# Layernorms computed beside attention: statistics, scalings and turns gathered at query tiles 1 to 5 of two heads each, and x of the second batch loaded in four groups

## The chip, the cores and the metric

The kernel runs on one core of one Trainium2 chip. The metric is the device time of one execution in microseconds (us), the median over several runs. A smaller time is better.

## What is computed

One transformer block in float32 with adaptive layernorms, on x of 2 batches x 1024 rows x 256 columns. Six vectors per batch (a shift, a scale and a gate for each of the two halves) come from a small product with the conditioning vector.

```
h = layernorm(x) * (1 + ca) + sa
x = x + ga * attention(h)        # 16 heads of 128, rotary q and k, causal softmax, output product with Wo
h = layernorm(x) * (1 + cb) + sb
x = x + gb * ffn(h)              # 256 -> 704 (silu gate * up) -> 256, weights int32 minus 128, scaled
```

There are four layernorms in all: first ("a") and second ("b") of each batch. Layernorm a of batch 0 stands ahead of everything, b of batch 1 behind everything. The two in the middle, a of batch 1 and b of batch 0, are computed while the attention of other heads runs. These two are what the change is about.

## The kernel before, in words

**Units.** The attention runs in 32 units, one for each head of each batch (`units`, line 592): units 0 to 15 are the heads of batch 0, units 16 to 31 those of batch 1. The loop over units (line 695) holds a loop over the eight query tiles i of 128 rows (line 701). The order of the instructions on every engine is the order in which this code issues them; nothing is reordered behind it (`manual_schedule`, line 646).

**One query tile i of a unit.** TensorE first multiplies an attention output of an earlier head with Wo (`project_out`, L509), and VectorE adds the result into x (L512); there is a single PSUM buffer for this product, so the next one has to wait until VectorE has taken it. Then come the scores of the tile against keys 0 to i (`score`, L422). VectorE adds the mask and takes the row maximum (L425), ScalarE takes the exponential (`expo`, L442). VectorE then turns the probabilities of the tile before, i - 1, in blocks of 32 x 32 (`turned`, L456); those of a unit's tile 7 are turned at tile 0 of the next unit. At tiles 1, 3, 4 and 6 TensorE also projects a half of q or k of the next unit (`project_qk`, L379). ScalarE turns half of it round (L391), GpSimd multiplies and adds (L392, L398), VectorE adds the bias and multiplies by the cosine (L395, `release`).

**The turned probabilities travel.** Blocks of 32 x 32 are turned on VectorE; the exchange between partition groups is done by 16 DMAs for each half of the query tiles, issued from SP (L468). They start when tile 3 or tile 7 is turned. The value products (`values`, L483) of the second half of a unit begin at tile 5 of the next unit, right after that tile's scores, and those of the first half at tile 7 of its own unit.

**What runs beside it.** At the end of each tile the loop calls `extras(n, i)` (line 595), with n the unit. It issues weight folding on GpSimd, loads and scalings of the feed-forward weights, and the middle layernorms. The table `((14, 1, "a"), (30, 0, "b"))` (line 619) says that the first one is due in unit m = 14 and the second in unit m = 30. A layernorm of eight row tiles takes these steps:

- `ln_stats` (L185, L186): mean and variance of a tile, VectorE
- `ln_sqrt` (L190): one square root for all tiles, ScalarE; it needs another activation table than the exponential, so a table load stands ahead of it and ahead of the next exponential
- `ln_scale` (L198, L201): reciprocal, then subtraction and multiplication, VectorE
- `ln_move` (L228): a 32 x 32 turn, VectorE
- `ln_send` (L237): eight DMAs from SP at a time, 16 in all; `ln_shift` (L240): shift and scale, GpSimd

Before the change the statistics of the eight tiles are taken in unit m - 4 (10 and 26), one at each query tile 0 to 7. The square root comes at query tile 1 of unit m - 3 (11 and 27). A scaling is issued at each of tiles 2 to 7 of that unit and 0 and 1 of unit m - 2 (12 and 28); each turn comes one query tile after its scaling. The x of batch 1 is loaded by ScalarE's DMA queue, in two groups of four single tiles, at tile 7 of units 4 and 8 (`load_x`, L64).

Of the kernel before, what the change touches and what calls it, by code (L numbers as in the profile page):

```python
# [21 lines left out]
NT = S // P  # L22
# [15 lines left out]
def adaln_block(ctx: ExitStack, tc: tile.TileContext, a, cos_d, sin_d, out):  # L38
    nc = tc.nc
# [23 lines left out]
    def load_x(b, t, n, eng):  # L63
        eng.dma_start(x[b][:, t : t + n, :], x_d[b, :, t : t + n, :])  # L64
# [47 lines left out]
    def modulation(which, pool, tag):  # L112

        pm = pool.tile([P, 512], F32, tag=tag, name=f"pm{which}")
        for n in range(2):
            for f in range(KC):
                at = (n * KC + f) * B
                for k in range(KC):
                    nc.tensor.matmul(
                        pm[:, at : at + B],  # L120
                        wmod[:, which // 2, k, n * D + f * P : n * D + (f + 1) * P],
                        sc[:, :, k],
                        start=(k == 0),
                        stop=(k == KC - 1),
                    )
                if not which:
                    warm_up(1)
        pms[which] = pm
# [3 lines left out]
    def shift_scale(which):  # L132
        pm = pms[which]
        for n in range(2):
            nc.vector.tensor_scalar(
                modT[:, which + n].rearrange("p f b -> p (f b)"),
                pm[:, n * KC * B : (n + 1) * KC * B],
                float(n),
                None,
                ALU.add,  # L140
            )
# [36 lines left out]
    def ln_stats(b, name, t):  # L178
        if t == 0:
            stats[b, name] = (  # L180
                small.tile([P, NT, 2], F32, tag="mv", name=f"mv_{name}{b}", bufs=2),
                small.tile([P, NT], F32, tag="rstd", name=f"rstd_{name}{b}", bufs=2),
            )
        st = small.tile([P, 6], F32, tag="st", name=f"st_{name}{b}_{t}")
        nc.vector.bn_stats(st, x[b][:, t, :])  # L185
        nc.vector.bn_aggr(stats[b, name][0][:, t, :], st)  # L186

    def ln_sqrt(b, name, t0, t1):
        mv, rstd = stats[b, name]
        nc.scalar.activation(rstd[:, t0:t1], mv[:, t0:t1, 1], AF.Sqrt, bias=eps_t)  # L190
# [3 lines left out]
    def ln_scale(b, name, blk, part=range(4)):  # L194
        mv, rstd = stats[b, name]
        part = [4 * blk + j for j in part]
        some = slice(part[0], part[-1] + 1)
        nc.vector.reciprocal(rstd[:, some], rstd[:, some])  # L198
        for t in part:
            xn = xnp.tile([P, D], F32, tag="xn", name=f"xn_{name}{b}_{t}")  # L200
            nc.vector.tensor_scalar(  # L201
                xn, x[b][:, t, :], mv[:, t, 0:1], rstd[:, t : t + 1], ALU.subtract, ALU.mult
            )
            xns[b, name, t] = xn
# [16 lines left out]
    def ln_move(b, name, t):  # L221

        if t == 0:
            moved[b, name] = [
                fpool.tile([P, 4, NB, KC, 4, 32], F32, tag="f", name=f"xt{n}_{name}{b}") for n in range(2)
            ]

        nc.vector.transpose(  # L228
            moved[b, name][0][:, :, t // 4, :, t % 4, :].rearrange("p c f q -> p f c q"),
            xns[b, name, t].rearrange("p (f c a) -> p f c a", c=4, a=32),  # L230
        )

    def ln_send(b, name, cs):
        src, dst = moved[b, name]
        for c in cs:
            for r in range(4):
                nc.sync.dma_start(dst[ts(c, 32), r], src[ts(r, 32), c])  # L237

    def ln_shift(b, name, blk, which, dest, f):
        nc.gpsimd.tensor_scalar(  # L240
            dest[:, f, :].rearrange("p (j r q) -> p r j q", j=4, q=32),
            moved[b, name][1][:, :, blk, f],
            modT[:, which + 1, f, b : b + 1],
            modT[:, which, f, b : b + 1],
            ALU.mult,
            ALU.add,
        )
# [10 lines left out]
    def ffn_scale_load():  # L258
        t = fpool.tile([P, 2 * HID], F32, tag="f", name="s_bc")
        nc.scalar.dma_start(t, a["scales"][:, : 2 * HID].to_broadcast([P, 2 * HID]))  # L260
        sbc.update(gate=t[:, :FULL], up=t[:, FULL : 2 * FULL], last=t[:, 2 * FULL :])

    def ffn_weight_load(n):
        if n == "gate":
            t = fpool.tile([P, KC * 2 * HID], I32, tag="f", name="raw")
            at = 0
            for m, w in (("gate", FULL), ("up", FULL), ("last", P)):
                raws[m] = t[:, at : at + KC * w].rearrange("p (k h) -> p k h", k=KC)
                at += KC * w
        nc.scalar.dma_start(raws[n], a[f"wq_{n}"])  # L270

    def ffn_weight_scale(n, k):
        nc.vector.scalar_tensor_tensor(
            wT[n][:, k, :], raws[n][:, k, :], -ZERO_POINT, sbc[n], ALU.add, ALU.mult
        )

    def ffn_down_load():
        raws["down"] = fpool.tile([P, NF, D], I32, tag="f", name="raw_down")
        nc.scalar.dma_start(raws["down"], a["wq_down"])
        sbc["down"] = xnp.tile([P, D], F32, tag="xn", name="s_down")  # L280
        nc.scalar.dma_start(sbc["down"], a["scales"][:, 2 * HID :].to_broadcast([P, D]))

    def ffn_down_scale(b, c):

        if c == 0:
            sd = sbc["down", b] = xnp.tile([P, D], F32, tag="xn", name=f"sd{b}")
            nc.vector.tensor_tensor(sd, sbc["down"], gate["b", b], ALU.mult)
        nc.vector.scalar_tensor_tensor(
            wdT[b][:, c : c + 2, :],
            raws["down"][:, c : c + 2, :],  # L290
            -ZERO_POINT,
            sbc["down", b].unsqueeze(1).to_broadcast([P, 2, D]),
            ALU.add,
            ALU.mult,
        )
# [27 lines left out]
    def fold_out(b, g):  # L323
        t = weights[b, g]["o"]
        if b == 0:

            for h in range(HG):
                c = R_BV + g * HG + h
                bw = small.tile([P, D], F32, tag="bw", name=f"bw_{g}{h}", bufs=2)
                nc.gpsimd.tensor_scalar(bw, t[:, h, :], cols[:, c : c + 1], None, ALU.mult)  # L330
                nc.gpsimd.tensor_tensor(bvacc, bvacc, bw, ALU.add)

        for h in range(HG):
            nc.gpsimd.tensor_tensor(t[:, h, :], t[:, h, :], gate["a", b], ALU.mult)
# [260 lines left out]
    def extras(n, i):  # L595

        if i == (2 if n else 7) and units[n][2] == 0:
            fold_out(*units[n][:2])
        if n == 0 and i == 6:
            modulation(2, ps_a, "a")  # L600
            shift_scale(2)

        if n == 2 and i == 7:
            ffn_scale_load()
        for m, name in ((3, "gate"), (5, "up"), (6, "last")):
            if n == m and i == 7:
                ffn_weight_load(name)
            if n == m + 1 and i in (2, 5):
                ffn_weight_scale(name, i // 4)
        if n in (4, 8) and i == 7:  # L610
            for t in range(4):
                load_x(1, n - 4 + t, 1, nc.scalar)
        if n == 7 and i == 7:
            ffn_down_load()
        if n in (8, 9) and i in (1, 3, 5):
            ffn_down_scale(n - 8, i - 1)


        for m, b, name in ((14, 1, "a"), (30, 0, "b")):
            if n == m - 4:  # L620
                ln_stats(b, name, i)
            if n == m - 3 and i == 1:
                ln_sqrt(b, name, 0, NT)
            t = 8 * (n - m + 3) + i - 2
            if 1 <= t <= NT:
                ln_move(b, name, t - 1)
            if 0 <= t < NT:
                ln_scale(b, name, t // 4, (t % 4,))
            if n in (m - 2, m - 1) and i == 6:
                ln_send(b, name, ((0, 1), (2, 3))[n - m + 2])  # L630
            if n == m and i in (4, 5, 7):
                blk = i // 6
                if i != 5:
                    dest = (new_hT if b else new_h2)(b, blk)
                else:
                    dest = (hT if b else h2s)[b, blk]
                for f in {4: (0,), 5: (1,), 7: (0, 1)}[i]:
                    ln_shift(b, name, blk, 0 if b else 2, dest, f)
        if n == 14 and i == 5:
            bias_row()  # L640
        if n == 15:
            add_bias(0, i)
        if n == 20:
            add_bias(1, i)

    with tc.manual_schedule():
# [48 lines left out]
        for n, u in enumerate(units):  # L695
            b, g, h = u
# [142 lines left out]
```

## Time and profile before

| what | value |
|---|---|
| median of 3 runs | 1085.96 us (1085.74 to 1087.61) |
| the profiled execution's own time | 1085.72 us |
| its span, first to last instruction | 1083.9 us |
| granted TensorE clock | 1.000 |
| busy: TensorE, VectorE, ScalarE, GpSimd | 99%, 60%, 47%, 37% |
| start of unit 0's and of unit 31's scores | 24.2 us, 931.1 us |

In the profile PE is TensorE's matmuls, PEld its weight loads, DVE VectorE, ACT ScalarE, POOL GpSimd, SP the engine that only issues DMAs; L422 is line 422 of the kernel. The unit starts are the first score matmul of a unit: the score group has 768 records, 24 in each unit, in order of time. Offsets "after the unit's start" below count from there.

### The profile page before, as it was taken

The numbers are of one execution on the slowest core, as the hardware profiler recorded it, in microseconds if no ns is written. First come the engines' busy times: TensorE is split into PE (matmuls) and PEld (weight loads), VectorE is DVE, ScalarE is ACT, GpSimd is POOL, SyncE is SP. The second block draws the span as 40 slices with busy tenths as digits, with TensorE's granted clock in tenths as the row PEclk, the third lists the DMA queues.
The fourth block names the chain that finished last, engine by engine and source line by source line (L and its number), as shares of the span: only waits on it lengthen the run. The fifth ranks groups of instructions, "written<-read, shape, count | busy, mean of one in ns | idle before, by whom it ended". The sixth has DMA issues, their size and how long they took to land.

```text
span 1083.9 us, 12352 instructions
## 1 busy us (share of the span) xinstructions
PE 1072.0 (99%) x3524; PEld 638.7 (59%) x3524; DVE 655.5 (60%) x1422; ACT 507.6 (47%) x956; POOL 397.2 (37%) x364
## 2 busy tenths in 40 slices
PE   8999999999999999999999999999999999999998
PEld 5556555566666556556566666665655566555656
DVE  5566566767677856556656665666677766454321
ACT  4645445455445444445455444454445445652110
POOL 4635353535343343664343433333333334100000
PEclk9999999999999999999999999999999999999999
DMA  6355656657564556555564645454556556422001
GB/s 211 81 140 132 159 141 137 168 116 182 127 150 96 131 120 151 126 128 143 111 148 106 151 109 141 101 138 101 142 117 153 117 123 143 97 66 51 20 20 39
DMA packets 67191, 130.97 MB, mean 121 GB/s; under 512 B 18962, under 2 KB 23314, under 8 KB 67124
## 3 DMA queue, kind: packets, MB, share of 16 engines
q1 hardware_dynamic: 64772, 125.91, 49.1%
q10 hardware_dynamic: 2304, 4.16, 1.2%
q8 instruction: 28, 0.46, 0.2%
q14 instruction: 39, 0.32, 0.1%
q0 software_dynamic: 48, 0.13, 0.1%
HBM read 25.26 MB, written 2.10 MB: 25 GB/s over the span
## 4 chain that ended last, share of the span: by engine, by line
PE 95%; DVE 2%; SPq 1%; DMA 1%; ACT 1%; issue 0%; DVEq 0%; ACTq 0%
PE po L483 23%; PE ps L422 22%; PE pk L379 10%; PE pq L379 10%; PE py L509 10%; PE pv L361 10%; PE pgu L538 6%; PE pd L566 3%; SPq L468 1%; DMA pT<-t 1%; DMA wmod<-in_wmod 0%; PE pd L575 0%; ACT L557 0%; DVE ps L425 0%; DVE t L456 0%
## 5 line engine op out<-in xcount | busy, mean ns | idle before, releaser
L442 ACT ACTIVATE p<-ps,nmax 128x128 f32<-128x128 f32 (+7 forms) x256 | 189.8, 741 | 421.6 <-DVE nmax L425 421.5
L422 PE MATMUL ps<-kT,qT 128*128 128x512 f32 (+3 forms) x768 | 289.5, 486 | 0.7 <-ACT p L442 0.7
L425 DVE CUSTOM_DVE_ANT_0 ps<-ps,mask 128x128 f32<-128x128 f32 (+7 forms) x256 | 195.6, 764 | 132.9 <-PE ps L422 132.6
L483 PE MATMUL po<-pT,v 128*128 128x512 f32 (+3 forms) x768 | 264.0, 487 | 1.7 <-DMA pT<-t 1.6
L512 DVE SCALAR_TENSOR_TENSOR x<-py,rden,x 128x256 f32<-128x256 f32 x256 | 123.0, 482 | 182.9 <-PE py L509 176.2
L483 PEld LDWEIGHTS po<-pT,v 128*128 128x128 f32 x768 | 145.2, 190 | 133.0 <-issue 107.5
L456 DVE STREAM_TRANSPOSE t<-p 128x128 f32<-128x128 f32 (+7 forms) x256 | 198.1, 774 | 0.4 <-ACT p L442 0.4
L422 PEld LDWEIGHTS ps<-kT,qT 128*128 128x128 f32 x768 | 145.7, 190 | 77.5 <-issue 62.9
L392 POOL TENSOR_TENSOR r_k<-r_k,sin_t 128x512 f32<-128x512 f32 x64 | 81.4, 1272 | 223.0 <-ACT r_k L391 222.9
L509 PE MATMUL py<-wo,o 128*128 128x256 f32 x512 | 151.5, 380 | 1.4 <-DVE x L512 1.4
L392 POOL TENSOR_TENSOR r_q<-r_q,sin_t 128x512 f32<-128x512 f32 x64 | 81.7, 1276 | 140.3 <-ACT r_q L391 137.3
L398 POOL TENSOR_TENSOR kT<-kT,r_k 128x512 f32<-128x512 f32 x64 | 81.3, 1270 | 140.9 <-DVE rden L506 101.5
L509 PEld LDWEIGHTS py<-wo,o 128*128 128x128 f32 x512 | 92.3, 190 | 67.3 <-issue 51.2
L361 PE MATMUL pv<-wv,hT 128*128 128x256 f32 x512 | 121.0, 379 | 1.1 <-DVE qT L395 1.1
L379 PE MATMUL pq<-hT,wq 128*128 128x512 f32 x256 | 120.6, 593 | 0.5 <-DVE hT L217 0.5
L379 PE MATMUL pk<-hT,wk 128*128 128x512 f32 x256 | 120.3, 592 | 0.0
L361 PEld LDWEIGHTS pv<-wv,hT 128*128 128x128 f32 x512 | 94.9, 190 | 19.9 <-DVE qT L395 1.2
L391 ACT ACTIVATE r_q<-pq,cols 64x512 f32<-64x512 f32 x128 | 87.4, 683 | 20.9 <-PE pq L379 19.2
L398 POOL TENSOR_TENSOR qT<-qT,r_q 128x512 f32<-128x512 f32 x64 | 83.6, 1306 | 31.1 <-DVE qT L395 28.6
L391 ACT ACTIVATE r_k<-pk,cols 64x512 f32<-64x512 f32 x128 | 87.4, 683 | 6.2 <-PE pk L379 0.4
L379 PEld LDWEIGHTS pk<-hT,wk 128*128 128x128 f32 x256 | 48.6, 190 | 54.6 <-issue 44.0
L379 PEld LDWEIGHTS pq<-hT,wq 128*128 128x128 f32 x256 | 46.1, 190 | 33.8 <-issue 31.2
(89 smaller groups left out, 688.8 us busy)
## 6 DMA issues: line engine op xcount, KB each, us to landing
pT<-t SPq DMA_DIRECT2D x512, 128.0 KB, 2.4
pT<-t SPq DMA_DIRECT2D x512, 64.0 KB, 2.0
wq<-in_Wq SPq DMA_DIRECT2D x16, 256.0 KB, 3.1
wk<-in_Wk SPq DMA_DIRECT2D x16, 256.0 KB, 4.0
wv<-in_Wv SPq DMA_DIRECT2D x16, 256.0 KB, 4.2
wo<-in_Wo SPq DMA_DIRECT2D x16, 256.0 KB, 2.9
out<-yo SPq DMA_DIRECT2D x16, 128.0 KB, 1.8
x<-in_x SPq DMA_DIRECT2D x4, 256.0 KB, 5.4
```

Of the source, the lines that this page charges most:

```text
L361: nc.tensor.matmul(pv[:, ts(j, HG * DH)], hT[b, n][:, k, ts(r, P)], weights[b, g]["v"][:, k, :], start=(k == 0), stop=(k == KC - 1),)
L379: nc.tensor.matmul(pq, weights[b, g][s][:, k, ts(h, DH)], hT[b, n][:, k, :], start=(k == 0), stop=(k == KC - 1),)
L391: nc.scalar.activation(r1[to], pq[of], AF.Identity, bias=cols[of, c : c + 1])
L392: nc.gpsimd.tensor_tensor(r1, r1, sin_t[:, sl], ALU.mult)
L398: nc.gpsimd.tensor_tensor(dst[:, sl], dst[:, sl], r1, ALU.add)
L422: nc.tensor.matmul(ps[:, c:e], qT[:, ts(i, P)], kT[:, c:e], start=True, stop=True)
L425: nc.vector.tensor_tensor_reduce(ps[:, :L], ps[:, :L], mask[:, NT - 1 - i :, :].rearrange("p t k -> p (t k)"), -SCALE, FLT_MAX, ALU.add, A ...
L442: nc.scalar.activation(p[:, :L], ps[:, :L], AF.Exp, bias=nmax, scale=-1.0, accum_out=dens[u][:, i : i + 1])
L456: nc.vector.transpose(t32[blk][:, :, j, : i + 1, :].rearrange("p c k b -> p k c b"), p[:, : (i + 1) * P].rearrange("p (k c a) -> p k c a", ...
L483: nc.tensor.matmul(po[:, off * P :], vs[b, g][:, k, ts(h, DH)], pT[:, off:, :, k, :], start=(k == 0), stop=(k == last),)
L509: nc.tensor.matmul(py[:, :D], outs[u][:, ts(t, P)], weights[b, g]["o"][:, h, :], start=True, stop=True)
L512: nc.vector.scalar_tensor_tensor(x[b][:, t, :], py[:, :D], rdens[u][:, t : t + 1], x[b][:, t, :], ALU.mult, ALU.add)
```

## The change

It moves the steps of the two middle layernorms inside `extras` and regroups the loads of x. Nothing is added to the work itself: the same number of statistics, scalings and turns of the same shapes.

- Statistics: at query tiles 1 to 4 of units m - 5 and m - 4 (9 and 10; 25 and 26), four row tiles in each.
- Square root: at query tile 6 of unit m - 4 (10; 26).
- Scalings: at query tiles 1 to 4 of units m - 3 and m - 2 (11 and 12; 27 and 28).
- Turns: at query tiles 2 to 5 of these units, each issued ahead of the scaling at the same query tile.
- x of batch 1: four DMAs of two tiles each, at tile 7 of units 0, 4, 6 and 8, in place of eight DMAs of one tile.

```diff
-        if n in (4, 8) and i == 7:
-            for t in range(4):
-                load_x(1, n - 4 + t, 1, nc.scalar)
+        if n in (0, 4, 6, 8) and i == 7:
+            load_x(1, max(0, n - 2), 2, nc.scalar)
...
         for m, b, name in ((14, 1, "a"), (30, 0, "b")):
-            if n == m - 4:
-                ln_stats(b, name, i)
-            if n == m - 3 and i == 1:
+
+            j = i - 1 if n in (m - 5, m - 3) else i + 3
+            if n in (m - 5, m - 4) and 1 <= i <= 4:
+                ln_stats(b, name, j)
+            if n == m - 4 and i == 6:
                 ln_sqrt(b, name, 0, NT)
-            t = 8 * (n - m + 3) + i - 2
-            if 1 <= t <= NT:
-                ln_move(b, name, t - 1)
-            if 0 <= t < NT:
-                ln_scale(b, name, t // 4, (t % 4,))
+            if n in (m - 3, m - 2) and 2 <= i <= 5:
+                ln_move(b, name, j - 1)
+            if n in (m - 3, m - 2) and 1 <= i <= 4:
+                ln_scale(b, name, j // 4, (j % 4,))
             if n in (m - 2, m - 1) and i == 6:
                 ln_send(b, name, ((0, 1), (2, 3))[n - m + 2])
```

## The prediction

> **What bounds the kernel now.** I read the page first, then the busy times of single units, then TensorE's waits, then the chain of work through the two units with the longest gaps.
>
> ```profile
> span 1083.9 us, 12352 instructions
> ...
> PE 1072.0 (99%) x3524; PEld 638.7 (59%) x3524; DVE 655.5 (60%) x1422; ACT 507.6 (47%) x956; POOL 397.2 (37%) x364
> ```
>
> TensorE sets the time. All that a reordering on the other engines can win is TensorE's gaps. So I cut the span at each unit's first score matmul and asked for busy times: unit 16 (a plain one), then 11, 12, 27, 28.
>
> ```profile
> core 0: us, PE busy (x) PEld busy (x) DVE busy (x) ACT busy (x) POOL busy (x), PEclk, DMA share, GB/s
> 489.80:519.07 29.27, 29.27 (x97) 17.61 (x96) 17.78 (x39) 14.09 (x27) 12.18 (x11) 1.00 0.49 111
> 340.68:370.05 29.37, 29.37 (x98) 17.53 (x97) 23.74 (x55) 16.93 (x32) 10.16 (x8) 1.00 0.58 143
> 370.05:400.95 30.90, 29.77 (x97) 17.37 (x96) 21.19 (x49) 14.24 (x29) 14.69 (x14) 1.00 0.53 118
> 811.81:841.30 29.49, 29.49 (x98) 17.53 (x96) 23.73 (x55) 16.92 (x32) 10.16 (x8) 1.00 0.59 143
> 841.30:872.51 31.21, 29.78 (x97) 17.37 (x96) 21.19 (x49) 14.25 (x29) 11.47 (x10) 1.00 0.53 117
> ```
>
> A plain unit takes 29.27 us with no gap. Unit 12 takes 1.63 more, unit 28 1.94 more, unit 27 0.22, unit 11 0.10. Of the other units with 96 matmuls only unit 5 (29.88, 0.61 more), 9 (0.10) and 15 (0.27) stand out. That is the whole prize: 3.57 us in units 12 and 28, 0.32 in 11 and 27, 0.98 elsewhere. What TensorE waited for:
>
> ```profile
> PE po L483 <- DMA pT<-t: 1.6, 3, 0.8
> PE py L509 <- DVE x L512: 1.4, 2, 0.7
> ```
>
> The two waits for x are at 372.84 (unit 12) and 844.09 (unit 28); the three for pT in units 5, 12 and 28 (0.37, 0.45, 0.75 us idle). The chain through unit 12:
>
> ```profile
> 369.91 0.63 DVE kT L395
> 370.55 0.35 DVE xt_a L228
> 370.90 0.06 DVE rstd_a L198
> 370.95 0.03 issue
> 370.98 1.13 DVE xn_a L201
> ...
> 372.30 0.50 DVE x L512
> ...
> 372.84 0.70 PE py L509 x2
> ...
> 384.92 1.97 DMA pT<-t
> 386.89 0.01 issue
> 386.90 3.67 PE po L483 x8
> ```
>
> The turn and the scaling issued at tile 7 of unit 11 (xt_a, xn_a) hold VectorE for 1.6 us at the start of unit 12, where a tile is short. The addition into x ends late, its single PSUM buffer comes free late, TensorE loses about 0.95 us (0.68 idle and a longer restart). Behind it waits the turn of unit 11's last probabilities: its first DMA is issued 4.16 us after the unit's start, against 2.60 in unit 16; the last of 16 is issued at 14.18 against 12.04 and lands at 16.72 against 14.45. A plain unit reaches the value product at 15.29; unit 12, late already, at 16.25, and waits again.
>
> **What the Trainium skill says.** "SBUF — State Buffer", Who interferes with whom: a VectorE tensor_scalar from SBUF to SBUF may take the port pair that it shares with GpSimd, and whichever comes second blocks wholly. The trace agrees: xn takes 0.41 us alone and 1.13 at 370.98, ending 0.15 after GpSimd's kT (370.69 to 371.96). "ScalarE: Activation LUTs", What ACT_TABLE_LOAD costs: 1283 ns and a drain of 1380. The trace shows 1283 and no such drain (12 to 19 ns between load and activation); the trace decides. "DMA: Bandwidth & Descriptors", Issuing engines are not separate DMA queues: ScalarE's loads share the DMA engines with SP's. In the trace, a 704 KB load by ScalarE at the end of unit 2 leaves unit 3's last pT landing at 14.46.
>
> **Part by part.** Timings within a unit are from the start of a unit.
>
> *Statistics.* Each is 0.40 + 0.18 = 0.59 us of VectorE, 16 in all, unchanged. Gone from tile 7 of units 10 and 26, where one delays the first pT DMA to 3.13 in units 11 and 27 (landings 15.01 and 15.13). Since unit 14 lost 0.26 with a landing at 15.25, the room over 14.45 is about 0.6. Added to tiles 1 to 4 of units 9 and 25. Unit 9 scales down-weights there (0.38 + 0.69 at tile 1, 0.65 at tile 3). At tile 1 that work ends at 4.76, +0.59 is 5.35; the next addition was due at 5.16 and the next mask at 5.81, so 0.2 is absorbed. At tile 3 10.59 becomes 11.2, the addition ends at 11.8, the mask is due at 12.05. Cost zero; with that cover gone, 0.59 a tile.
>
> *Square root.* 1.28 + 0.30 + 1.28 us of ScalarE, moved from tile 1 of unit 11, where it pushes an exponential from 6.5 to 9.1 without a TensorE gap, to tile 6 of unit 10. There ScalarE is free from 25.32 to 28.27. The root ends at 26.93. The load back for the exponential either runs at once (28.22: free), or stands behind the exponential's wait for the maximum (28.21), and then the exponential of tile 7 is 1.28 late. The trace has both: a load at 940.51 went ahead of its wait, one at 936.72 idled 1.59 behind it. The second has the separate semaphore instruction that every plain exponential here has, so I take it. Queued behind are a copy and tile 0's exponential (0.5 late). The score bank is needed at 2.38 and free at 1.4. VectorE turns the last tile at about 1.55 instead of 1.06, so the first pT DMA goes at 3.1: as late as the statistics made it before. Units 11 and 27 gain nothing (bounds: 0.32 gained to 0.3 lost).
>
> *Scalings and turns.* Tiles 6, 7 and 0 are relieved. In units 12 and 28 the first pT DMA goes back to 2.60, the first wait (0.95 each) disappears, and the product waits only if transfers are slow. New slots: at tile 1 VectorE is free from 3.73 to 5.23 and GpSimd idle, scaling 0.13 + 0.41: hidden. At tile 2: 0.42 turn, 0.13, and a scaling that GpSimd's L398 (to 8.86) holds to 9.0: the same end as in unit 11 before, without a gap. At tile 3 as unit 11 had it, but in unit 12 weight folding on GpSimd may hold the scaling until 11.9: the mask starts 0.4 late. At tile 4 as before (15.7). At tile 5 a turn alone. Behind these scalings waits the turn of tile 3, and so the pT of the first half: landing 25.05 in plain units, needed at 26.68, so 0.4 is covered by 1.4 of room; past that each us costs a us. The 16 SP sends keep their place, after all turns; SP has issued its 16 of that half by then.
>
> Unit 12 then: 1.63 gained. Unit 28: SP lost 1.03 there on one DMA issue (1.62 against 0.59), when a 16 KB packet of the instruction queue was under way (848.06, 1.14 us). The page has 28 such packets; 7048 matmuls and weight loads over 256 give 27.5, so I take them for TensorE's instructions and expect them at the same place. That costs between 0 (unit 9 bore one, landing 15.17) and 0.9; I take unit 14's 0.26 as nearest, say 0.2. Unit 28 gains 1.94 - 0.2 = 1.74. Unit 5's pT wait has such a packet too (174.17) and stays.
>
> *Loads of x.* ScalarE's queue loses four issues of 0.44 and gets none at a busy place: its sequencer issues them under the exponential. A 256 KB load beside units 1 and 7 is less than the 704 KB of unit 3: zero; bounds 0.1 gained (unit 9) to 0.3 lost (unit 1, start-up).
>
> **Sum.** 1085.72 - 1.63 - 1.74 = 1082.35 for the profiled execution (span 1080.5 and the same 1.8 around it). It stood 0.24 under the median, so 1085.96 - 3.37 = 1082.6.
>
> **Rivals.**
> 1. *More comes back.* The table load goes ahead (0.32), and unit 5 and 9 clear up because four DMAs of x no longer precede them (0.71): with 0.2 in unit 28 that is 4.6, 1081.4. Against: unit 5's loads had landed by 4.6, the delay begins at 8.2.
> 2. *Only the first waits go.* If pT is set by DMA traffic and not by VectorE's start, TensorE arrives earlier and waits longer at the product: gain near zero, 1085.9. Against: the first issue itself is 1.56 late in units 12 and 28. For: unit 28's slow issue.
> 3. *Slower.* Scalings packed into tiles 2 to 4 delay the turn of tile 3 beyond its room of 1.4 in all four units. Gains are 3.4, so it is slower than before when the delay passes 1.4 + 0.85 = 2.25 per unit. Three blocked scalings add 2.2 at most (0.72 each), three turns 1.25: at 3.1 all told, four times 1.7 - 3.4 = 3.4 lost, 1089.4. Against: idle gaps at those tiles take up most, and unit 11 had the same load at tiles 2 to 4 and its turn of tile 3 was on time (12.80).
>
> **How the numbers follow.** Forecast 0.68, own range 1081.9 to 1083.8 (unit 28 keeping up to 0.9, or 0.3 lost beside units 11 and 27); rival 1 0.17; rival 2 0.10; rival 3 0.05. A measurement can tell 0.2%, 2.17 us, from no change: faster is under 1083.79. The forecast but for 0.02, and rival 1, lie there: faster 0.83. Rival 2 and the 0.02: same 0.12. Slower 0.05. A range of 1081.0 to 1084.0 leaves out rivals 2 and 3 and a little more.
>
> **What would show it.** Right: units 12 and 28 at 29.3 and 29.5; no wait of py for x in mid-kernel; the first pT DMA at 2.60 in units 12 and 28 and 3.1 in 11 and 27; an exponential of tile 7 starting near 29.5 in units 10 and 26; unit 5 still 29.88. Wrong: a new wait at tile 7 of units 11, 12, 27, 28, pT landing after 15.1 in unit 12, or a gap in unit 1 or 9.

## The result and the profile after

| kernel | median, 13 runs | span of its profiled execution | that execution's own time |
|---|---|---|---|
| before | 1085.84 us (1084.2 to 1087.61) | 1083.9 | 1085.72 |
| after | 1082.51 us (1081.34 to 1084.78) | 1082.9 | 1084.72 |

The ratio is 0.997, with an interval of 0.9962 to 0.9978: 3.3 us faster, against 3.4 forecast. The profiled execution after is one of the slowest of its 13, only 1.0 us under the one before. That matters below.

The busy times of the units shown before, now in the changed kernel (unit 16, then 11, 12, 27, 28, and after them 19 and 24):

```profile
core 0: us, PE busy (x) PEld busy (x) DVE busy (x) ACT busy (x) POOL busy (x), PEclk, DMA share, GB/s
488.30:517.57 29.27, 29.27 (x97) 17.61 (x96) 18.03 (x39) 14.35 (x29) 12.23 (x11) 1.00 0.50 112
341.01:370.29 29.28, 29.28 (x98) 17.61 (x96) 22.48 (x51) 15.42 (x30) 10.17 (x8) 1.00 0.59 143
370.29:399.59 29.30, 29.30 (x97) 17.53 (x96) 21.68 (x51) 14.35 (x29) 14.81 (x14) 1.00 0.55 122
812.02:841.29 29.27, 29.27 (x97) 17.61 (x96) 22.47 (x51) 15.41 (x30) 10.18 (x8) 1.00 0.61 144
841.29:871.53 30.24, 29.51 (x97) 17.53 (x96) 22.50 (x51) 14.36 (x29) 11.58 (x10) 1.00 0.55 122
576.12:606.06 29.94, 29.51 (x98) 17.53 (x97) 18.11 (x39) 14.35 (x29) 10.12 (x8) 1.00 0.58 141
723.15:753.47 30.32, 29.51 (x97) 17.53 (x96) 18.11 (x39) 14.35 (x29) 11.49 (x10) 1.00 0.47 104
```

Units 11, 12 and 27 are plain units now, within 0.03 us. Unit 28 still takes 0.97 more. Units 19 and 24, which hold no layernorm work, take 0.67 and 1.05 more, which they did not before. TensorE's waits for the value product's input and for other engines say the same:

```profile
PE po L483 <- issue: 1.5, 2, 0.8
...
PE po L483 <- DMA pT<-t: 0.8, 3, 0.4
```

There is no line for py and x any more. The five waits of po are in units 5, 14, 19, 24 and 28. (The two put down to "issue" have the late pT DMAs too: the last ones land 15.96 and 15.88 us after the start of units 24 and 28, where a plain unit has 14.4.)

The chain through unit 12 is TensorE alone:

```profile
370.02 0.43 PE py L509 x2
370.45 0.22 PE ps L422 x2
370.67 1.73 PE pv L361 x8
372.40 0.43 PE py L509 x2
372.83 0.43 PE ps L422 x2
...
385.74 3.47 PE po L483 x8
```

No piece of VectorE or of a DMA stands in it, where xt_a, xn_a, x and pT stood before. The spans add up: units 12, 28, 27, 11, 9, 15 and 5 are shorter by 1.60, 0.97, 0.22, 0.09, 0.10, 0.27 and 0.16, in sum 3.41; units 24, 19, 1 and 14 are longer by 1.05, 0.67, 0.62 and 0.12, in sum 2.46. The difference of 0.95 is that of the spans. So one profile places the gain in units 12 and 28, but it does not measure the gain: that is what the medians are for.

### The profile page after: what moved, and what is told of

It is laid out like the page before. It is cut to its first block, busy times and chain, and to the rows that moved or that the text cites. A ratio compares the mean times of both kernels' runs of the same rounds, so it can differ in the third digit from the quotient of the medians.

```text
span 1082.9 us, 12350 instructions
## 1 busy us (share of the span) xinstructions
PE 1071.2 (99%) x3524; PEld 638.8 (59%) x3524; DVE 655.9 (61%) x1422; ACT 508.0 (47%) x956; POOL 397.2 (37%) x364
## 3 DMA queue, kind: packets, MB, share of 16 engines
q10 hardware_dynamic: 1728, 4.16, 1.1%
## 4 chain that ended last, share of the span: by engine, by line
PE 95%; DMA 1%; SPq 1%; DVE 1%; ACT 1%; issue 0%; POOL 0%; DVEq 0%; ACTq 0%
PE po L483 23%; PE ps L422 22%; PE pv L361 10%; PE pq L379 10%; PE pk L379 10%; PE py L509 10%; PE pgu L538 6%; PE pd L566 3%; DMA pT<-t 1%; SPq L468 1%; DMA wmod<-in_wmod 0%; PE pd L575 0%; ACT L557 0%; PE ptx_b L210 0%; DVE t L456 0%
## 5 line engine op out<-in xcount | busy, mean ns | idle before, releaser
L398 POOL TENSOR_TENSOR kT<-kT,r_k 128x512 f32<-128x512 f32 x64 | 81.3, 1270 | 140.7 <-DVE rden L506 117.6
L398 POOL TENSOR_TENSOR qT<-qT,r_q 128x512 f32<-128x512 f32 x64 | 83.6, 1306 | 31.8 <-DVE qT L395 28.9
```

The costliest lines, as they stand in the source:

```text
L398: nc.gpsimd.tensor_tensor(dst[:, sl], dst[:, sl], r1, ALU.add)
```

## The experiments

My theory: the gain comes from VectorE being free at the end of tile 7 and at tile 0 of the next unit. Rivals: it comes from the regrouped loads of x; or from the earlier statistics and root; or the waits for pT are made by DMA traffic and not by VectorE. Ratios are to the kernel before on the same chip.

**loads_only.** The kernel before with the new loads alone.

```diff
-        if n in (4, 8) and i == 7:
-            for t in range(4):
-                load_x(1, n - 4 + t, 1, nc.scalar)
+        if n in (0, 4, 6, 8) and i == 7:
+            load_x(1, max(0, n - 2), 2, nc.scalar)
```

> The kernel before with nothing changed but the loads of x (four DMAs of two tiles). Theory, VectorE's relief at tiles 7 and 0: no gain, 1085.8 us, within 0.5 of the kernel before; units 12 and 28 still near 30.9 and 31.2 us. Rival, the regrouped loads clear ScalarE's queue and the DMA engines: 0.7 us or more gained, with units 5 and 9 at 29.3.

Measured: 1085.45 us, ratio 1.0004 (0.9995 to 1.0012). Units 12 and 28 take 30.98 and 31.33. Units 5 and 9 are at 29.27 in its profile, but units 19, 24 and 14 have grown. The loads bring nothing. They cost something in unit 1: it takes 31.41 here and 31.13 before. The load at tile 7 of unit 0 is under way from 22.8 to 26.0 us after that unit's start, beside the last pT transfers, which land at 26.20 instead of 24.69. TensorE wants them at 26.27 (5.09 us into unit 1), and its product starts 0.2 after the landing, so 0.13 late. The loss of 0.27 here lies inside the bound of 0.3 that the prediction kept for it; that of the changed kernel's profile does not, as shown below.

**stats_root.** The changed kernel with scalings and turns at their old places.

```diff
-            if n in (m - 3, m - 2) and 2 <= i <= 5:
-                ln_move(b, name, j - 1)
-            if n in (m - 3, m - 2) and 1 <= i <= 4:
-                ln_scale(b, name, j // 4, (j % 4,))
+            t = 8 * (n - m + 3) + i - 2
+            if 1 <= t <= NT:
+                ln_move(b, name, t - 1)
+            if 0 <= t < NT:
+                ln_scale(b, name, t // 4, (t % 4,))
```

> The changed kernel with scalings and turns put back to their old query tiles (2 to 7, and 0 to 2 of the next unit); statistics, root and loads stay as changed. Theory: nearly all of the gain is gone, 1085.5 us; units 12 and 28 wait for the addition into x again (0.7 us idle) and for pT. Rival, the earlier root or the statistics bring the gain: 1082.5 us kept. ScalarE's exponential of tile 7 in unit 10 is 1.3 us late in both.

Measured: 1085.0 us, ratio 0.9994 (0.9985 to 1.0003). Both waits for the addition into x are back, 0.68 us each:

```profile
PE py L509 <- DVE x L512: 1.4, 2, 0.7
```

The first pT DMA of units 12 and 28 goes at 4.16 and 4.17 again. So the scalings and turns carry the gain, by difference: they were not moved alone. Statistics, root and loads together bring too little to measure, though units 11 and 27 keep their 0.31 us in this profile.

**tile7_dose.** The changed kernel with dummy work at tile 7: a turn after units 16 to 19, a turn and a scaling after units 20 to 23.

```diff
+        if 16 <= n <= 23 and i == 7:
+            dt = xnp.tile([P, D], F32, tag="xn", name=f"dt_{n}")
+            nc.vector.transpose(dt, cos_t[:, :D])
+            if n >= 20:
+                ds = xnp.tile([P, D], F32, tag="xn", name=f"ds_{n}")
+                nc.vector.tensor_scalar(
+                    ds, cos_t[:, :D], eps_t[:, 0:1], eps_t[:, 0:1], ALU.subtract, ALU.mult
+                )
```

> The changed kernel with dummy VectorE work at query tile 7: one 32x32 turn of 128x256 in units 16 to 19 (0.42 us), a turn and a scaling in units 20 to 23 (1.6 us if GpSimd holds the scaling). They write tiles that nobody reads. Theory: the units after the small dose (17 to 20) stay at 29.27 us, where no instruction fetch meets pT; those after the large dose (21 to 24) wait for the addition into x and take 0.9 us more each, the first pT DMA at 4.1 us; the product at tile 5 adds no wait, since TensorE is itself late. Rival, the wait for pT is set by DMA traffic: no difference between the two groups, first pT DMA at 2.6 in both.

Measured (one run): busy times of unit 18, after a turn, and of units 22 and 23, after a turn and a scaling:

```profile
546.18:575.46 29.28, 29.28 (x98) 17.61 (x96) 18.23 (x40) 14.23 (x29) 11.49 (x10) 1.00 0.49 108
664.42:694.65 30.23, 29.55 (x97) 17.45 (x96) 19.46 (x41) 13.95 (x29) 11.48 (x10) 1.00 0.47 105
694.65:724.94 30.29, 29.61 (x97) 17.45 (x96) 19.46 (x41) 14.50 (x29) 10.11 (x8) 1.00 0.57 139
...
PE py L509 <- DVE x L512: 2.7, 4, 0.7
```

All four units 21 to 24 wait 0.68 to 0.71 us for x, units 17 to 20 do not wait. The first pT DMA goes at 2.8 to 3.2 after the small dose and at 4.2 after the large one. Unit 24 waits 0.71 for pT as well. The cause is made and unmade at will here, with no layernorm in sight. There is room for the small dose: 0.42 us costs 0.04 at most. The large one is 0.42 and 1.29 us, and costs 0.95 to 1.11 in units 21 to 23.

**tile7_lock.** What makes the large dose so long? In it the scaling came second. Here it comes first in units 16 to 19, and two turns replace the pair in units 20 to 23.

```diff
+        if 16 <= n <= 23 and i == 7:
+            if n < 20:
+                ds = xnp.tile([P, D], F32, tag="xn", name=f"ds_{n}")
+                nc.vector.tensor_scalar(
+                    ds, cos_t[:, :D], eps_t[:, 0:1], eps_t[:, 0:1], ALU.subtract, ALU.mult
+                )
+            for r in range(1 if n < 20 else 2):
+                dt = xnp.tile([P, D], F32, tag="xn", name=f"dt_{n}{r}")
+                nc.vector.transpose(dt, cos_t[:, :D])
```

> The changed kernel with other dummy VectorE work at query tile 7: in units 16 to 19 the scaling ahead of the turn, in units 20 to 23 two turns, results read by nobody. Theory, what tips the stall is the scaling held by GpSimd's addition into k: a scaling that comes first starts before that addition does and takes 0.41 us, so the work is 0.84 us in both groups, the first pT DMA goes at 3.4 us or sooner and the units lose at most 0.2 us each at the addition into x. Rival, any work of a turn and a scaling at this place costs the 0.95 us that tile7_dose showed.

Measured (one run): the four scalings take 401 ns each; in tile7_dose they took 1285 to 1287 (duration in ns, least, median and most; first this run, then tile7_dose):

```profile
L642 DVE TENSOR_SCALAR ds<-cos_t,eps_t x4: 401/401/401, 518.7 to 607.5; 128x256 f32<-128x256 f32 x4
...
L644 DVE TENSOR_SCALAR ds<-cos_t,eps_t x4: 1285/1286/1287, 634.8 to 725.7; 128x256 f32<-128x256 f32 x4
```

No wait for x. Units 18, 21 and 22 take 29.30, 29.49 and 29.35, the others 29.3 to 29.5, but for unit 19: it loses 0.79 at pT, where its first pT DMA goes at 3.56 and a 16 KB packet comes 9.9 us into the unit. In the other units the first pT DMA goes at 3.25 to 3.28. The same turn and scaling cost 0.95 and more in one order, and 0.2 or less in the other with unit 19 left out: what decides is whether GpSimd's addition into k (L398) stands ahead of the scaling, which makes 0.84 us of VectorE into 1.7.

**scale_first.** That suggests a cheaper edit to the kernel before: swap the two in every slot.

```diff
-            if 1 <= t <= NT:
-                ln_move(b, name, t - 1)
             if 0 <= t < NT:
                 ln_scale(b, name, t // 4, (t % 4,))
+            if 1 <= t <= NT:
+                ln_move(b, name, t - 1)
```

> The kernel before with one thing changed: in each slot the scaling is issued ahead of the turn of the tile before. All places stay. Theory: at tile 7 of units 11 and 27 the scaling (after its reciprocal) starts just before GpSimd's addition into k at 0.64 us and takes 0.41 in place of 1.13; VectorE reaches the addition into x some 0.7 us sooner in units 12 and 28, which leaves at most 0.3 us of each first wait and takes 0.6 us off the start of pT: 1083.5 us. Rival: the reciprocal's wait makes the scaling miss that moment, GpSimd is first and nothing changes: 1085.7.

Measured: 1085.84 us, ratio 1.0002 (0.9993 to 1.001). The rival was right. The timeline at the start of unit 12 shows why:

```profile
368.88 0.71 DVE L395 SCALAR_TENSOR_TENSOR kT<-pk,cols,cos_t 128x512 f32<-128x512 f32 x1
...
369.50 0.15 DVE L198 RECIPROCAL rstd_a<-rstd_a 128x1 f32<-128x1 f32 x1
369.69 1.46 DVE L201 TENSOR_SCALAR xn_a<-x,mv_a,rstd_a 128x256 f32<-128x256 f32 x1
369.73 1.27 POOL L398 TENSOR_TENSOR kT<-kT,r_k 128x512 f32<-128x512 f32 x1 [3.96 <-DVE rstd_a L198]
371.07 0.43 DVE L228 STREAM_TRANSPOSE xt_a<-xn_a 128x256 f32<-128x256 f32 x1
```

The reciprocal ahead of it delays the scaling to 0.04 us before GpSimd's addition. That is not enough: the scaling ends 0.15 us after the addition, having taken 1.46 us, and the wait for x grows from 0.68 to 1.01. The hold is 0.33 us longer than in the kernel before (1.13), and so is the wait: in this pair TensorE loses what VectorE loses, once the room is used up. In tile7_lock the scaling had started 0.23 us ahead.

**late_after.** What is left of the waits for pT? The value product is moved away from them.

```diff
-                if i in (1, 3, 4, 6) and nxt:
-                    project_qk(nxt, *{1: ("q", 0), 3: ("k", 0), 4: ("q", 1), 6: ("k", 1)}[i])
-                if i in (5, 6) and prev:
-                    values(prev, 1, 4 * (i - 5), 4 * (i - 4))
+                if i in (1, 3, 4, 5) and nxt:
+                    project_qk(nxt, *{1: ("q", 0), 3: ("k", 0), 4: ("q", 1), 5: ("k", 1)}[i])
+                if i == 6 and prev:
+                    values(prev, 1, 0, 8)
```

> The changed kernel with the second-half value product moved from tiles 5 and 6 to tile 6 alone, and the second projection of k from tile 6 to tile 5: the same TensorE work in another order, the product begins some 3.7 us later. Theory, what is left of TensorE's waits for pT in mid-kernel comes from packets of TensorE's own instruction fetch that delay SP's DMAs by up to 1.1 us: all waits of po for pT in units 2 to 30 disappear, 1081.0 us. Rival, the moved work makes tile 6 too long or VectorE late at tile 5: 1082.5 or slower, with waits on the score bank or on ps_a.

Measured: 1082.21 us, ratio 0.997 (0.9962 to 0.9978). The waits for pT at this product are gone in all units, but a new one stands in unit 14:

```profile
PE pbias L341 <- DVE qT L395: 1.5, 1, 1.5
```

The bias product at tile 5 needs a PSUM buffer that q's second half still holds.

**late_fix, late_fix_again.** late_after with the bias product one tile later; the second is a repeat beside late_before_fix.

```diff
-        if n == 14 and i == 5:
+        if n == 14 and i == 6:
             bias_row()
```

> late_after with the bias product issued at tile 6 of unit 14 in place of tile 5, so that it need not wait for the PSUM buffer of q's second half. Theory: that wait of 1.45 us goes and nothing takes its place: 1080.7 us, the fastest of all. Rival: VectorE is late at tile 6 and the wait returns there: 1082.2.

> late_fix once more, on the same chip as late_before_fix. Both theories: 1080.6 us.

Measured: 1080.59 us, ratio 0.9955 (0.9942 to 0.9969), and 1081.3 us, ratio 0.9958 (0.9946 to 0.9971). The new wait is gone. By its ratio this is the fastest version, 1.3 to 1.6 us ahead of the change, but the intervals overlap, so the runs alone do not settle that it is ahead.

**late_before.** The same move of the product in the kernel before.

> The kernel before with the second-half value product moved to tile 6 alone and the second projection of k to tile 5. Theory: units 12 and 28 keep their first wait (addition into x, 0.95 us each) and lose the second one (pT); the waits for pT in other units go as well; unit 14 gains a wait of the bias product, 1.6 us, as in late_after; so 1084.0 us, 1.9 above late_after. Rival, both waits are one and the same delay handed down: units 12 and 28 at 29.3 us, level with late_after.

Measured: 1081.78 us, ratio 0.9965 (0.9953 to 0.9978). A miss: both waits of units 12 and 28 disappeared, not one. In its trace the projection of k, one tile earlier now, has taken two things away from the end of tile 7. VectorE's cosine step for k (0.71 us) is done already, and GpSimd's addition into k too, so the scaling takes 0.41. The work ahead of the addition into x ends 0.69 us after the start of unit 12 (369.29), not at 2.06:

```profile
369.08 0.40 DVE L228 STREAM_TRANSPOSE xt_a<-xn_a 128x256 f32<-128x256 f32 x1
...
369.29 0.38 PE L422 MATMUL ps<-kT,qT 128*128 128x128 f32 x2
...
369.56 0.41 DVE L201 TENSOR_SCALAR xn_a<-x,mv_a,rstd_a 128x256 f32<-128x256 f32 x1
```

The wait of unit 12 had three parts ahead of it, then, and the change took two of them (the turn and the scaling) where this move took the third and the hold by GpSimd. The projection and the product were never moved apart: that the first wait went with the projection and the second with the product is read from the trace, not tested.

**late_before_fix.** late_before with the bias product at tile 6.

> late_before with the bias product at tile 6 of unit 14, so late_fix with the layernorms and the loads of x where the kernel before had them. Theory, corrected: the change and the later product remove the same waits, so the layernorms' places are worth nothing once the product is late: 1080.7 us, level with late_fix within 0.5, units 12 and 28 at 29.3. Rival: places still matter and it is 1 us or more behind late_fix.

Measured: 1080.85 us, ratio 0.996 (0.9946 to 0.9973), level with late_fix_again; units 12 and 28 at 29.27. Once the product is late, the change is worth nothing that can be measured. Both cure one crowded place.

**pad48.** Is the packet that delays SP one of TensorE's instructions? 48 more of them ahead of everything:

```diff
-    for n in range(3):
-        warm_up(4)
+    for n in range(15):
+        warm_up(1)
```

> The changed kernel with the three wide warm-up products at the start made into fifteen narrow ones: 48 more TensorE instructions ahead of everything, at most 0.5 us at the start. Theory, the packets of 16 KB are TensorE's instructions: each one comes some 7 us earlier in its unit, so the slow SP issues and waits for pT leave units 5, 14, 24 and 28 and appear in units out of 6, 10, 11, 15, 16, 20, 25, 29, 30, with the packets 7 to 11 us after those units' start. Rival, the packets belong to SP or come at a fixed time: the same units as before, 5, 14, 19, 24, 28.

Measured (one run, 1085.78 us): nearly as the theory had it. The page counts one packet more (first the changed kernel, then this run):

```profile
q8 instruction: 28, 0.46, 0.2%
...
q8 instruction: 29, 0.48, 0.2%
```

All other profiles count 28. With 7048 matmuls and weight loads, 28 packets are one for some 250 of these instructions. In the changed kernel the 16 KB packets stood 9.9, 4.8, 10.0, 9.5 and 4.5 us into units 5, 14, 19, 24 and 28. Now those of 5, 14, 19 and 28 come 2.4 us into unit 5 or before the unit begins, and there are packets 4.5, 4.5, 9.6, 4.6 and 4.5 us into units 10, 15, 20, 24 and 29. Units 10, 20 and 24 wait for pT (0.66, 0.64, 0.76 us), units 15 and 29 lose 0.1; 5, 19 and 28 are clean. Unit 24 did not clear, because its packet moved from 9.5 to 4.6 only. Most packets came 5 to 12 us earlier and some hardly moved; the mean of the 24 in units 1 to 30 is 6.4 us, where 48 instructions are 7.3 us by the pace of a plain unit. Unit 14 waits 1.3 us without such a packet inside it: pT landed at 16.6. Ahead of it a packet at the end of unit 13 met SP's sends of the layernorm (one issue of 1.84 us) and the weight loads behind them; that this made pT late is my reading. The packets follow TensorE's instruction count, then. What sets the last few microseconds of their place stays open.

## Why the prediction was right, and where its terms were off

*Statistics.* No cost in units 9 and 25, as forecast: both at 29.27.

*Square root.* The mechanism was read rightly, with no drain between load and activation (11 to 13 ns in these traces where the activation has nothing else to wait for, a little less than the 12 to 19 given). The table load stood behind the wait for the maximum, in unit 10:

```profile
339.99 1.28 ACT L442 ACT_TABLE_LOAD   x1 [1.32 <-DVE nmax L425]
...
341.29 1.11 ACT L442 ACTIVATE p<-ps,nmax 128x1024 f32<-128x1024 f32 x1
...
342.52 1.25 DVE L456 STREAM_TRANSPOSE t<-p 128x1024 f32<-128x1024 f32 x1
```

The exponential starts 29.55 us after the unit's start; the prediction had 29.5. The term behind it was mis-sized: the turn of the last tile slips to 1.51 us, but from the 1.30 of nearly every unit, not from unit 16's 1.06, which I had taken. Unit 16 is the odd one in the profile before: the 2.60, 12.04 and 14.45 that the prediction gives for it are unit 17's, and its own are 2.37, 11.84 and 14.29. The first pT DMA goes at 2.82 and not at 3.1, so units 11 and 27 came out clean: 0.31 us gained where I had put zero.

*Scalings and turns.* The slots came out as worked: at tile 2 the scaling ends at 9.0, at tile 4 at 15.7 (15.2 in unit 12), the first half's pT lands at 25.25 in unit 12 and 25.65 in 28, against 26.68. In unit 12 the wait for x and the wait for pT are gone, 1.60 of 1.63. At tile 3 of unit 12 the scaling took 0.41, not the blocked time I had allowed, so the mask was 0.2 late and not 0.4. The profile shows weight folding (L330) under way on GpSimd from 0.32 us before this scaling to 0.25 after it: as far as GpSimd's times can be trusted, the blocking that the prediction cites did not show here, so not every GpSimd instruction holds a scaling.

*Unit 28.* Here a term was off by much: I kept 0.2 us for the slow SP issue there, and it cost 0.97 in this execution; in tile7_dose and tile7_lock 0.8. The issue took 2.01 us with the packet 4.5 us into the unit. I had taken unit 14's 0.26 as the nearest row, one value of something that varies: by the start of its product unit 14 lost 0.4 (after) and 1.4 us (loads_only) in other profiles, and unit 9, given as a case of no loss, had lost 0.10.

*Loads of x.* I had put zero, with 0.3 lost in unit 1 as the bound. In the changed kernel's profile unit 1 loses 0.62, outside the bound. About 0.3 of it is the loss that loads_only shows. The rest comes at tile 7: an SP issue 17.5 us into the unit takes 2.12 us beside a 16 KB packet, where two issues near this place took 0.78 and 0.90 before, and the first half's pT lands at 28.79 instead of 27.43.

*Units that the change does not touch.* I left these waits as they were and expected the 16 KB packets at the same place. That did not hold. TensorE has the same instructions ahead of units 19 and 24 as before, but their packets came 10.0 and 9.5 us into the unit, among the pT issues of the second half, and not at 15.9 and 15.7, among those of the first half, which have room. Other profiles agree: unit 19 loses 0.64 and 0.67 where its packet stands near 10 (loads_only, after), and nothing where it stands near 16 (before, scale_first, stats_root). Units 5, 14, 19 and 24 together lose 1.7 us more in this execution than in the one before. It is the likely reason why single executions lie 3.4 us apart in both kernels; the runs without profile can't show it.

*The sum.* That 3.3 came so close to 3.4 is in part luck. As far as one profile tells, the terms are 1.60 (unit 12), 0.97 (unit 28) and 0.31 (units 11 and 27) gained and 0.62 (unit 1) lost, 2.3 in all and not 3.4. By its interval the gain is 2.4 to 4.1 us. What it has beyond 2.3 is not traced to a term, and one profile of 13 executions cannot do so.

*Rivals.* Only the first waits go: refuted, both went in unit 12. More comes back: the 0.3 us of units 11 and 27 did, but not by its cause (the load did not go ahead), and unit 5 cleared by 0.16 only. Slower: no delay at tile 3 came near 2.25 us.

## What to carry to other kernels

When one engine is busy 99% of the time, cut the span into the units of the loop and compare each with a plain one: the few tenths of a percent that can be won are whole microseconds in two or three units, and the work that delays them sits at the shortest tile, not where the busy shares are high. Put side work into slots where the bound engine's tile is long and the neighbour engine is idle, and look at what the helper shares with a third engine: the same two instructions cost 0.95 us or 0.2 by their order against a GpSimd addition. Before packing more finely, ask whether the consumer can come later: moving the value product a tile later, with the projection of k and the bias product moved to suit, gave at least as much as the whole reordering, and made it needless.

## What the runs showed of the hardware that I had not expected

- Instruction packets pass through the DMA queues and get in the way of SP. In the traces before and after, from unit 1 on, every SP issue of pT over 0.66 us, in place of 0.59, overlaps such a packet; with one of 16 KB (0.9 to 1.7 us) it lasts up to 2.1 us, and pT transfers in flight take up to 4.3 us to land in place of 2.4.
- A VectorE scaling that began 0.04 us before a GpSimd addition (L398) by the profile's times was held until 0.15 us after its end (1.46 us); one that began 0.23 us ahead was not (0.40 us).
- A scaling during which the profile shows GpSimd's weight folding (L330) under way was not held (0.41 us).
